# How the first expert gets its rows: gathered from DRAM and turned, or picked out of the resident tiles by one-hot products

## The chip, the cores and the metric

The kernel runs on one core of a Trainium2 chip. A core has five engines with a queue each: TensorE (PE, matrix products; its weight loads are listed apart as PEld), VectorE (DVE), ScalarE (ACT), GpSimd (POOL) and SyncE (SP), and 16 DMA engines. SP issues most of the transfers, and POOL those that need indices or go to late places. The metric is the time of one execution on the device in microseconds (us); lower is better.

## The reference

625 nodes with 768 features go through a layer norm, two graph attention convolutions over 20000 edges and a residual. What the change touches is in the transformer block after it (n = 625 rows, E = 8 experts, K = 1, hidden size 3072):

```python
h = _ln(x, ln1_g, ln1_b)
q, k, v = (jnp.einsum('btd,hds->bhts', h, w) for w in (Wq, Wk, Wv))
scores = jnp.where(causal, jnp.einsum('bhts,bhus->bhtu', q, k) * d ** (-0.5), -jnp.inf)
out = jnp.einsum('bhtu,bhus->bhts', jax.nn.softmax(scores, axis=-1), v)
x = x + out.transpose(0, 2, 1, 3).reshape(b, t, d) @ Wp + bp
h2 = _ln(x, ln2_g, ln2_b).reshape(-1, d)
w, sel = jax.lax.top_k(h2 @ Wg, K)
w = jax.nn.softmax(w, axis=-1)
combine = jnp.zeros((n, E)).at[jnp.arange(n)[:, None], sel].add(w)
hid = jax.nn.relu(jnp.einsum('nd,edf->enf', h2, W1) + b1[:, None, :])
y = jnp.einsum('enf,efd->end', hid, W2) + b2[:, None, :]
return x + jnp.einsum('ne,end->nd', combine, y)
```

(three lines for q, k and v are drawn together here). With K = 1 the weight is a softmax over one value, so it is 1: each row goes through the one expert with its largest gate logit. The kernel computes only that expert for each row, in f32.

## The kernel before, in words

**Tiles.** The 625 rows are T = 5 tiles of R = 125 rows on partitions. D = 768 is KD = 6 blocks of 128. An expert's weights come in NFC = 3 pieces for each layer: `w1[c]` (128 x 6 x 1024) and `w2[c]` (128 x 8 x 768), 3.1 MB each, in two transfers each (`load_piece`, L1300 for the first layer and L1309 for the second). There is one set of these six tiles, so a piece is loaded when the products that read its predecessor are done.

**Attention to gate.** After attention, `project(t, i, cs)` (L1092) multiplies the turned attention output by half i of Wp and adds it to the residual `xx`; `second_norm` (L1113) makes the normalised tile `h2[:, t, :]` (its last DVE operation is L1121). `gate_turn` (`tile_turned`, L1076) turns that tile and `gate` (L1134) multiplies it by Wg; `choose` takes the best expert `ef` and the one-hot row `oh`. `choose_first` counts tile 0's experts. The most frequent one is the **first expert** (`origin`, `first`).

**Routing.** `send(t)` (L1177) counts each row's place within its expert (`pk`, then `rank` and `slot` on DVE), makes its position `pos = expert * RE + slot` (RE = 640, slot from Q = 32 up, L1188) and scatters the rows of `h2` to the DRAM buffer `xg` by an indirect DMA on POOL (L1170). `send_sums` does the same for the residual sums, into `xr`, with the node's number in a last column.

**The first expert ahead of the loop.** While tiles 3 and 4 are not through, the first expert is run on up to B = 128 rows of it from the first TA = 3 tiles. POOL gathers these rows from `xg` into `xa` (L1269) behind the scatters of the three tiles. PE turns `xa` in six blocks with a column stride of 6 (`turn_rows`, L1086), into two PSUM tiles (`tpx`, four and two blocks), copied to `xaT` by DVE and ACT (L1088). This stands behind `gate(3)` and the last products of `project(4, ...)`. POOL also gathers the residual sums into `ra` (L1279), first read when the bias is added (L1424). `first_step` (L1443) then runs the expert with the helpers of `Wide`: `into(c)` (L1372) makes 512 hidden columns in 24 product records, `turn` (L1383, L1388) turns them and adds bias and relu, `out_of(c)` (L1398) multiplies them into the two PSUM banks `pw`. `add_up` adds these to the rows (L1435), `scatter_out` writes them (L1439).

**The loop.** All other rows, in blocks: a table, made on DVE meanwhile, has for each block its expert and kind. The number of blocks is `nblk`. `tc.For_i` (L1695) is a loop on the device, each engine with its own counter. In a block a branch runs `Wide.begin` (the first layer) for 64 or 128 rows, another the narrow form for up to 32 rows (`narrow`, L1649), and then `finish` runs `Wide.end` (the second layer), `add_up` and the scatter. So for wide blocks the branch of the narrow form lies between the two layers.

**What sets the order.** The orders of PE (from attention on), DVE and ACT (from L1228) and SP (L950 to L1694) are the order in which the program is written (`tc.manual_schedule`). Each engine works its queue in order and waits at an instruction until what that reads or overwrites is ready. On SP the loads of the first expert's second and third pieces stand first (L1605 to L1609); then the first loop block's expert word is read, and its loads go out (`load_first`, `load_second`, `load_bias`), then the block count is read into a register on every engine (L1693), and the loop is entered.

Of the kernel before, what the change touches and what calls it, by code (L numbers as in the profile page):

```python
# [9 lines left out]
F32 = mybir.dt.float32  # L10
# [5 lines left out]
OP = mybir.AluOpType  # L16
# [5 lines left out]
R = 125  # L22
T = N // R
XR = 120
D = 768
KD = D // 128
# [17 lines left out]
B = 128  # L44
NS = E + N // B
# [3 lines left out]
Q = 32  # L49
U = B // Q + 1  # L50
TA = 3
RE = 640
# [17 lines left out]
def gnn_moe_kernel(ctx: ExitStack, tc: tile.TileContext, p, out):  # L70
    nc = tc.nc
# [4 lines left out]
    small = ctx.enter_context(tc.tile_pool(name="small", bufs=4))  # L76
# [4 lines left out]
    xg = dram.tile([NR, D], F32, name="xg")  # L81
# [7 lines left out]
                   pattern=[[R, T]], base=0, channel_multiplier=1)  # L89
# [15 lines left out]
    def part(w, k, c, i, n):  # L105
# [4 lines left out]
    ident = const.tile([128, 128], F32, name="ident")  # L110
# [11 lines left out]
                            base=0, channel_multiplier=-1)  # L122
# [32 lines left out]
    with tc.tile_pool(name="gnn", bufs=1) as gp:  # L155
# [37 lines left out]
        with tc.tile_pool(name="oneh", bufs=12) as op_, \  # L193
# [33 lines left out]
            def etile(shape, name, dtype=F32):  # L227
# [4 lines left out]
                           allow_small_or_imprecise_dtypes=True)  # L232
# [399 lines left out]
        with tc.tile_pool(name="gw", bufs=2, reuse_waits="tile") as gw, \  # L632
# [121 lines left out]
            def project(t):  # L754

                for i in range(2):
                    ph = psum_half()
                    for c in range(KH):
                        nc.tensor.matmul(ph[:R, :384], h1T[:, c, cols(t)], part(w2, KH, c, i, 384),  # L759
                                         start=(c == 0), stop=(c == KH - 1))  # L760
                    nc.scalar.copy(xl2[:, t, i * 384:(i + 1) * 384], ph[:R, :384])
                for s, b in enumerate((as2, ad2)):
                    junk = gw.tile([R, HC], F32, tag="hw", name="junk")
                    nc.vector.scalar_tensor_tensor(junk[:, :D], xl2[:, t, :], 1.0, b, op0=OP.mult,
                                                   op1=OP.mult, accum_out=al2[:, s, t, 0:1])
# [97 lines left out]
    with tc.tile_pool(name="att", bufs=1, reuse_waits="tile") as a1, \  # L863
# [58 lines left out]
        for t in range(T):  # L922
# [1 line left out]
            with tc.high_priority() if t < T - 1 else nullcontext():  # L924
                hw = first_norm(t)
            turn(hT, hw, KD, t)
        xa = sx.tile([B, D], F32, tag="xa", name="xa")
        ra = sx.tile([B, D + 1], F32, tag="ra", name="ra")


# [147 lines left out]
                nc.scalar.copy(dst[:, k:k + 3, :], tp[:, :3 * R].rearrange("p (k t) -> p k t", k=3))  # L1078
            return dst

        def turn_rows(dst, src, ps, part, copy):

            k0, k1 = ((0, 4), (4, KD))[part]
            tp = ps.tile([128, 512], F32, tag="tp", name="tpx").rearrange("p (k r) -> p k r", k=4)
            for k in range(k0, k1):
                nc.tensor.transpose(tp[:, k - k0, :],  # L1086
                                    src.rearrange("p (d k) -> p k d", k=KD)[:, k], ident)
            return copy(dst[:, k0:k1, :], tp[:, :k1 - k0, :])  # L1088

        po, stats = {}, {}  # L1090
# [39 lines left out]
        def gate(t):  # L1130
            h2T = h2Ts.pop(t)
            pl = ps.tile([128, 512], F32, tag="tp", name="pl")
            for c in range(KD):
                nc.tensor.matmul(pl[:R, :E], h2T[:, c, :], wg[:, c, :],  # L1134
                                 start=(c == 0), stop=(c == KD - 1))
            nc.vector.tensor_copy(lg[:, t, :], pl[:R, :E])
            choose(t)
# [5 lines left out]
        nc.gpsimd.iota(io8, pattern=[[1, E]], base=0, channel_multiplier=0,  # L1143
                       allow_small_or_imprecise_dtypes=True)
        origin = ap.tile([R, 1], F32, name="origin")

        def best(a):
            mx = small.tile([R, 8], F32, name="mx")
# [9 lines left out]
        def choose_first():  # L1158

            pc = ps.tile([128, 512], F32, tag="tp", name="pc")  # L1160
            nc.tensor.matmul(pc[:R, :E], ones, oh[:, 0, :], start=True, stop=True)
            c0 = small.tile([R, E], F32, name="c0")
            nc.vector.tensor_copy(c0, pc[:R, :E])
            nc.vector.tensor_copy(origin, best(c0))
            nc.vector.tensor_copy(first, origin[0:1, :])

        scatters = {}

        def scatter(buf, src, t):
            s = nc.gpsimd.indirect_dma_start(  # L1170
                out=buf, out_offset=bass.IndirectOffsetOnAxis(ap=pos[t], axis=0),
                in_=src, in_offset=None)
            for q in scatters.setdefault(id(buf), []):
                tc.declare_no_dep(s.ins, q.ins, reason="other rows")
            scatters[id(buf)].append(s)

        def send(t):  # L1177

            pk = ps.tile([128, 512], F32, tag="tp", name="pk")
            for s in range(t + 1):  # L1180
                nc.tensor.matmul(pk[:R, :E], before if s == t else ones, oh[:, s, :],
                                 start=(s == 0), stop=(s == t))
            rank = small.tile([R, E], F32, name="rank")
            slot = small.tile([R, 1], F32, name="slot")
            nc.vector.tensor_tensor_reduce(rank, pk[:R, :E], oh[:, t, :], scale=1.0, scalar=0.0,
                                           op0=OP.mult, op1=OP.add, accum_out=slot)
            nc.vector.tensor_scalar_add(slot, slot, float(Q))
            nc.vector.scalar_tensor_tensor(pos[t], ef[:, t:t + 1], float(RE), slot, op0=OP.mult,  # L1188
                                           op1=OP.add)
            scatter(xg, h2[:, t, :], t)  # L1190

        def send_sums(t):
            nc.vector.tensor_add(x[:, t, :], x[:, t, :], xx[:, t, :])
# [72 lines left out]
        project(3, 1, (2, 3, 4))  # L1266
        send(2)
        first_e = nc.values_load(first[0:1, 0:1], engines=[SP, pool], min_val=0, max_val=E - 1)
        nc.gpsimd.dma_start(xa, xg[ds(first_e * RE + Q, B), :])  # L1269
        for i in range(2):  # L1270
            project(3, i, (KD - 1,))
        turn_probs(last, latest, 1, True)
# [5 lines left out]
            send_sums(t)  # L1278
        nc.gpsimd.dma_start(ra, xr[ds(first_e * RE + Q, B), :])  # L1279
        project(4, 1, most)  # L1280
        gate(3)
        for i in range(2):
            project(4, i, (KD - 1,))
        for part in range(2):
            turn_rows(xaT, xa, ps, part, (nc.vector.tensor_copy, nc.scalar.copy)[part])
        whole_norm(4)
        pe_order.close()

# [23 lines left out]
    def load_bias(e, **cond):  # L1312
        nc.sync.dma_start(b2b, b2[ds(e, 1), :].to_broadcast([B, D]), **cond)
# [24 lines left out]
    def load_first(e, new):  # L1338

        with tc.manual_schedule(engines={SP}):  # L1340
            for c in range(NFC):
                load_piece(e, 0, c, cond=new)

    def load_second(e, new):

        with tc.manual_schedule(engines={SP}):
            for c in range(NFC):
                load_piece(e, 1, c, cond=new)

    class Wide:  # L1350
# [53 lines left out]
        def begin(self):  # L1404
            self.into(0)
            self.into(1)
            for c in range(2, self.n):
                self.turn(c - 2)
                mm = self.into(c)
            return mm  # L1410

# [272 lines left out]
    def word(i, *engines):  # L1684
        return nc.values_load(table[0:1, 0, ds(i, 1)], min_val=0, max_val=2047,
                              **(dict(engines=engines) if engines else {}))

    word_0 = word(0, SP)
    load_first((word_0 >> 8) & 7, (word_0 >> 7) & 1)
    load_second((word_0 >> 8) & 7, (word_0 >> 7) & 1)  # L1690
    load_bias((word_0 >> 8) & 7, cond=(word_0 >> 7) & 1)

    n_blk = nc.values_load(nblk[0:1, 0:1], min_val=1, max_val=NS)  # L1693
    sp_order.close()  # L1694
    with tc.For_i(0, n_blk, 1, iteration_sync="reg_based") as i:  # L1695
        w = word(i)
# [85 lines left out]
```

## Time and profile before

| | us |
|---|---|
| runs | 984.97, 987.18, 987.40; median 987.18 |
| the profiled execution | 986.62 |
| its span, first to last instruction | 984.7 |
| PE busy in 0 to 575 (graph, attention, gate) | 564.2 of 575 |
| PE busy in 575 to 649 (first expert) | 70.6 of 74 |
| PE busy in 649 to 985 (loop) | 314.7 of 336 |
| mean granted clock of TensorE | 0.993 of full |

The profile is one execution. Times in it are us from the span's start; a line number is that of the kernel before. A row of the timeline is a run of like instructions: start, length, engine, line, operation, output <- inputs, shape, count, and in brackets how long the engine was idle before it and what it waited for. An f32 product is recorded twice, as are its weight loads: the 6 products of `gate` are x12. Transposes are recorded once. `PEld`, `SPq`, `DVEq` and the like are weight loads and an engine's own sequencer. The granted clock is the share of full speed at which TensorE was allowed to run.

### The profile page before, as it was taken

The numbers are of one execution on the slowest core, as the hardware profiler recorded it, in microseconds if no ns is written. First come the engines' busy times: TensorE is split into PE (matmuls) and PEld (weight loads), VectorE is DVE, ScalarE is ACT, GpSimd is POOL, SyncE is SP. The second block draws the span as 40 slices with busy tenths as digits, with TensorE's granted clock in tenths as the row PEclk, the third lists the DMA queues.
The fourth block names the chain that finished last, engine by engine and source line by source line (L and its number), as shares of the span: only waits on it lengthen the run. The fifth ranks groups of instructions, "written<-read, shape, count | busy, mean of one in ns | idle before, by whom it ended". The sixth has DMA issues, their size and how long they took to land. (4 is left out here: it accounts for less than half of the span.)

```text
span 984.7 us, 15208 instructions
## 1 busy us (share of the span) xinstructions
PE 949.6 (96%) x4675; PEld 585.8 (59%) x4676; DVE 449.1 (46%) x1310; ACT 296.0 (30%) x776; POOL 65.0 (7%) x147
## 2 busy tenths in 40 slices
PE   8999999999999999999999989999999998999995
PEld 5555665777555556677775655546454656554653
DVE  8978892783384920485555644112111213221303
ACT  6897550562230110444442302101100121011302
POOL 2000000000000100000000113010101010210000
PEclk9999999999999999999999999999999999999998
DMA  9404103001500356999300699310789999999993
GB/s 269 179 1 172 34 1 144 1 1 49 112 1 1 98 144 124 416 400 383 120 1 1 227 346 335 87 43 9 274 291 325 361 366 409 341 396 378 407 404 138
DMA packets 87726, 191.69 MB, mean 195 GB/s; under 512 B 34404, under 2 KB 36316, under 8 KB 87673
## 3 DMA queue, kind: packets, MB, share of 16 engines
q1 hardware_dynamic: 80441, 175.22, 50.1%
q0 software_dynamic: 7152, 15.64, 5.1%
q8 instruction: 29, 0.48, 0.2%
q10 hardware_dynamic: 80, 0.16, 0.1%
q14 instruction: 24, 0.20, 0.1%
HBM read 213.29 MB, written 39.55 MB: 257 GB/s over the span
## 5 line engine op out<-in xcount | busy, mean ns | idle before, releaser
L1398 PE MATMUL pw<-ew,hT 128*64 128x384 f32 (+1 forms) x672 | 159.7, 487 | 4.4 <-DVE iq L1721 2.5
L1398 PEld LDWEIGHTS pw<-ew,hT 128*64 128x64 f32 (+1 forms) x672 | 100.5, 160 | 58.0 <-issue 12.8
L1372 PE MATMUL ph<-ew,xid 128*64 128x512 f32 (+1 forms) x432 | 127.7, 594 | 3.4 <-DMA ew<-in_L_ffn_W_dram 1.8
L1388 ACT ACTIVATE hT<-tph,bT 128x64 f32<-128x64 f32 (+1 forms) x168 | 41.0, 362 | 269.1 <-PE tph L1383 174.4
L1372 PEld LDWEIGHTS ph<-ew,xid 128*64 128x64 f32 (+1 forms) x432 | 53.6, 155 | 66.8 <-issue 59.8
L692 PE MATMUL agg<-xl,zT 125*125 125x256 f32 (+1 forms) x300 | 79.9, 417 | 2.9 <-ACT zT L681 2.9
L1375 DVE COPY hb<-ph 128x512 f32<-128x512 f32 x28 | 19.4, 692 | 137.1 <-PE ph L1372 137.1
L692 PEld LDWEIGHTS agg<-xl,zT 125*125 125x125 f32 x300 | 54.5, 188 | 21.4 <-ACT zT L681 4.4
L1435 DVE TENSOR_TENSOR rw<-rw,pw 64x192 f32<-64x192 f32 (+1 forms) x48 | 12.9, 315 | 90.4 <-PE pw L1398 90.0
L410 PE MATMUL pp<-w,yT 128*125 128x512 f32 x120 | 53.5, 595 | 0.2 <-ACT yT L396 0.2
L800 PE MATMUL ph<-wr,h1T 128*125 128x384 f32 x160 | 52.6, 486 | 0.0
L759 PE MATMUL ph<-w,h1T 128*125 128x384 f32 x160 | 52.4, 486 | 0.0
L256 ACT ACTIVATE step<-halved,past 125x210 f16<-125x210 f16 x138 | 50.9, 460 | 0.0
L1030 DVE CUSTOM_DVE_ANT_0 e<-sc,later 125x625 f32<-125x625 f32 (+4 forms) x60 | 29.9, 543 | 36.2 <-PE sc L1007 36.2
L174 PE MATMUL ph<-wr,yT 128*125 128x512 f32 x96 | 42.2, 594 | 1.0 <-ACT pr L419 0.9
L1034 ACT ACTIVATE e<-e,of 125x625 f32<-125x625 f32 (+4 forms) x60 | 35.7, 597 | 23.3 <-DVE of L1030 23.3
L759 PEld LDWEIGHTS ph<-w,h1T 128*125 128x125 f32 x160 | 30.0, 188 | 21.2 <-issue 0.5
L800 PEld LDWEIGHTS ph<-wr,h1T 128*125 128x125 f32 x160 | 29.8, 188 | 21.1
L1098 PE MATMUL po<-wpj,aT 128*125 128x384 f32 x120 | 41.7, 492 | 0.4 <-DVE xx L1102 0.4
L941 PE MATMUL pv<-L_ffn_Wv,hT 128*125 128x384 f32 x120 | 39.5, 486 | 0.0
L978 PE MATMUL pq<-hT,L_ffn_Wq 128*128 128x313 f32 (+1 forms) x144 | 39.4, 429 | 0.0
L978 PE MATMUL pq<-hT,L_ffn_Wk 128*128 128x313 f32 (+1 forms) x144 | 39.4, 429 | 0.0
(336 smaller groups left out, 1262.3 us busy)
## 6 DMA issues: line engine op xcount, KB each, us to landing
ew<-in_L_ffn_W_dram SPq DMA_DIRECT2D x108, 1536.0 KB
xr<-zt SPq DMA_DIRECT2D x5, 3076.0 KB
xg<-zt SPq DMA_DIRECT2D x5, 3072.0 KB
w<-in_L_gnn_W_dram SPq DMA_DIRECT2D x4, 1536.0 KB
wr<-in_L_gnn_Wr_dram SPq DMA_DIRECT2D x4, 1536.0 KB
xid<-xg POOLq DMA_DIRECT2D x40, 96.0 KB, 9.3
b2b<-in_L_ffn_b_dram SPq DMA_DIRECT2D x9, 384.0 KB
rw<-xr POOLq DMA_DIRECT2D x14, 192.2 KB
```

What stands on the lines that cost most here:

```text
L174: nc.tensor.matmul(pp[:R, :], yT[:, c, cols(t)], part(wr1, KD, c, i, 512), start=(c == 0), stop=(c == KD - 1))
L256: nc.scalar.activation(o, halved[:, :n], AF.Sign, bias=at, scale=-1.0)
L410: nc.tensor.matmul(pp[:R, :], yT[:, c, cols(t)], part(w1, KD, c, i, 512), start=(c == 0), stop=(c == KD - 1))
L692: nc.tensor.matmul(self.agg[:R, c0:c0 + n], zT[:, s, :], xl[:, s, x0:x0 + n], start=(s == 0), stop=(s == T - 1))
L759: nc.tensor.matmul(ph[:R, :384], h1T[:, c, cols(t)], part(w2, KH, c, i, 384), start=(c == 0), stop=(c == KH - 1))
L800: nc.tensor.matmul(ph[:R, :384], h1T[:, k, cols(t)], part(wr2, KH, k, i, 384), start=(k == 0), stop=(k == KH - 1))
L941: nc.tensor.matmul(pp[:R, :384], hT[:, c, cols(t)], w[i][:, c, :], start=(c == 0), stop=(c == KD - 1))
L978: nc.tensor.matmul(pp[:, :b - a], w[:, c, c0:c0 + 128], hT[:, c, a:b], start=(c == 0), stop=(c == KD - 1))
L1098: nc.tensor.matmul(po[t, i][:R, :384], aT[:, c, cols(t)], wpj[i][:, c, :], start=(c == 0), stop=(c == KD - 1))
L1372: mm = nc.tensor.matmul(ph[g * M:(g + 1) * M, :C].rearrange("p (j f) -> p j f", f=128), self.xT[:, k, :], w[:, k, g], start=(k == 0), stop ...
L1388: self.made = nc.scalar.activation(hT[c][:, k, r], tp[:, k, r], AF.Relu, bias=self.bT[:, f:f + 1])
L1398: mm = nc.tensor.matmul(pw[i][g * M:(g + 1) * M, :384], hT[c][:, k, g * M:(g + 1) * M], w[:, self.block(c, g, k), i * 384:(i + 1) * 384], ...
```

## The change

- `xa`, its gather and `turn_rows` go. `pick_rows` stands in their place: for each of the six strided column blocks, three products, one for each of the first three tiles, with the tile's rows of `h2` as weights and `chosen[:, t, :]` (125 x 128) as the moving operand. `chosen` has a one in row r and column c if row r of tile t is row c of the first expert, so the sum of the three products is the block of `xaT` that the turn gave. It stands ahead of `gate(3)`.
- For that, POOL writes a row of column numbers (`io_row`), `choose_first` computes the first expert's first position (`from_row`), and `send(t)` for t < 3 has three more DVE operations: the row's position again, less `from_row`, and the comparison with `io_row`.
- `Wide.begin` gets two 1 x 1 products, one into each bank of `pw`, ahead of its last `into`.
- On SP the block count is read ahead of the first loop block's loads, and the bias load goes ahead of those of the second layer.

```diff
--- before.py
+++ after.py
@@ -924,7 +924,6 @@
             with tc.high_priority() if t < T - 1 else nullcontext():
                 hw = first_norm(t)
             turn(hT, hw, KD, t)
-        xa = sx.tile([B, D], F32, tag="xa", name="xa")
         ra = sx.tile([B, D + 1], F32, tag="ra", name="ra")
 
 
@@ -1078,13 +1077,15 @@
                 nc.scalar.copy(dst[:, k:k + 3, :], tp[:, :3 * R].rearrange("p (k t) -> p k t", k=3))
             return dst
 
-        def turn_rows(dst, src, ps, part, copy):
+        def pick_rows(dst, part, copy):
 
             k0, k1 = ((0, 4), (4, KD))[part]
             tp = ps.tile([128, 512], F32, tag="tp", name="tpx").rearrange("p (k r) -> p k r", k=4)
             for k in range(k0, k1):
-                nc.tensor.transpose(tp[:, k - k0, :],
-                                    src.rearrange("p (d k) -> p k d", k=KD)[:, k], ident)
+                for t in range(TA):
+                    nc.tensor.matmul(tp[:, k - k0, :],
+                                     h2[:, t, :].rearrange("p (d k) -> p k d", k=KD)[:, k],
+                                     chosen[:, t, :], start=(t == 0), stop=(t == TA - 1))
             return copy(dst[:, k0:k1, :], tp[:, :k1 - k0, :])
 
         po, stats = {}, {}
@@ -1143,6 +1144,11 @@
         nc.gpsimd.iota(io8, pattern=[[1, E]], base=0, channel_multiplier=0,
                        allow_small_or_imprecise_dtypes=True)
         origin = ap.tile([R, 1], F32, name="origin")
+        from_row = ap.tile([R, 1], F32, name="from_row")
+        io_row = ap.tile([R, B], F32, name="io_row")
+        nc.gpsimd.iota(io_row, pattern=[[1, B]], base=0, channel_multiplier=0,
+                       allow_small_or_imprecise_dtypes=True)
+        chosen = ap.tile([R, TA, B], F32, name="chosen")
 
         def best(a):
             mx = small.tile([R, 8], F32, name="mx")
@@ -1163,6 +1169,7 @@
             nc.vector.tensor_copy(c0, pc[:R, :E])
             nc.vector.tensor_copy(origin, best(c0))
             nc.vector.tensor_copy(first, origin[0:1, :])
+            nc.vector.tensor_scalar(from_row, origin, float(RE), float(Q), op0=OP.mult, op1=OP.add)
 
         scatters = {}
 
@@ -1188,6 +1195,12 @@
             nc.vector.scalar_tensor_tensor(pos[t], ef[:, t:t + 1], float(RE), slot, op0=OP.mult,
                                            op1=OP.add)
             scatter(xg, h2[:, t, :], t)
+            if t < TA:
+                row = small.tile([R, 1], F32, name="row")
+                nc.vector.scalar_tensor_tensor(row, ef[:, t:t + 1], float(RE), slot, op0=OP.mult,
+                                               op1=OP.add)
+                nc.vector.tensor_sub(row, row, from_row)
+                nc.vector.tensor_scalar(chosen[:, t, :], io_row, row, None, op0=OP.is_equal)
 
         def send_sums(t):
             nc.vector.tensor_add(x[:, t, :], x[:, t, :], xx[:, t, :])
@@ -1266,7 +1279,6 @@
         project(3, 1, (2, 3, 4))
         send(2)
         first_e = nc.values_load(first[0:1, 0:1], engines=[SP, pool], min_val=0, max_val=E - 1)
-        nc.gpsimd.dma_start(xa, xg[ds(first_e * RE + Q, B), :])
         for i in range(2):
             project(3, i, (KD - 1,))
         turn_probs(last, latest, 1, True)
@@ -1278,11 +1290,11 @@
             send_sums(t)
         nc.gpsimd.dma_start(ra, xr[ds(first_e * RE + Q, B), :])
         project(4, 1, most)
+        for part in range(2):
+            pick_rows(xaT, part, (nc.vector.tensor_copy, nc.scalar.copy)[part])
         gate(3)
         for i in range(2):
             project(4, i, (KD - 1,))
-        for part in range(2):
-            turn_rows(xaT, xa, ps, part, (nc.vector.tensor_copy, nc.scalar.copy)[part])
         whole_norm(4)
         pe_order.close()
 
@@ -1406,6 +1418,10 @@
             self.into(1)
             for c in range(2, self.n):
                 self.turn(c - 2)
+                if c == self.n - 1:
+                    for bank in pw:
+                        nc.tensor.matmul(bank[:1, :1], ident[:, :1], ident[:, :1], start=True,
+                                         stop=True)
                 mm = self.into(c)
             return mm
 
@@ -1685,12 +1701,12 @@
         return nc.values_load(table[0:1, 0, ds(i, 1)], min_val=0, max_val=2047,
                               **(dict(engines=engines) if engines else {}))
 
+    n_blk = nc.values_load(nblk[0:1, 0:1], min_val=1, max_val=NS)
     word_0 = word(0, SP)
     load_first((word_0 >> 8) & 7, (word_0 >> 7) & 1)
+    load_bias((word_0 >> 8) & 7, cond=(word_0 >> 7) & 1)
     load_second((word_0 >> 8) & 7, (word_0 >> 7) & 1)
-    load_bias((word_0 >> 8) & 7, cond=(word_0 >> 7) & 1)
-
-    n_blk = nc.values_load(nblk[0:1, 0:1], min_val=1, max_val=NS)
+
     sp_order.close()
     with tc.For_i(0, n_blk, 1, iteration_sync="reg_based") as i:
         w = word(i)
```

## Prediction

> **What bounds the kernel now.** I read the page first, for the engine that is busy all through.
>
> ```profile
> PE 949.6 (96%) x4675; PEld 585.8 (59%) x4676; DVE 449.1 (46%) x1310; ACT 296.0 (30%) x776; POOL 65.0 (7%) x147
> ...
> PE   8999999999999999999999989999999998999995
> ...
> PEclk9999999999999999999999999999999999999998
> ```
>
> TensorE is busy 949.6 of 984.7 us in every slice: the end moves by what is added to its queue, by its idle time, and by its clock. The other engines count only where PE waits for them. So I went to the timeline of the stage that is edited (574 us, where the first expert's rows are fetched and turned):
>
> ```profile
> 571.49 1.37 PE L1134 MATMUL pl<-wg,h2T 128*125 128x8 f32 x12
> ...
> 571.74 0.61 POOL L1269 DMA_DIRECT2D xa<-xg  x1 [9.10 <-DMA xg<-h,pos]
> ...
> 572.72 1.53 PE L1098 MATMUL po<-wpj,aT 128*125 128x384 f32 x4
> ...
> 575.09 1.05 PE L1086 MATMUL tpx<-ident,xa 128*128 128x128 f32 x6 [0.84 <-DMA xa<-xg]
> ...
> 576.99 0.64 DVE L1088 COPY xaT<-tpx 128x512 f32<-128x512 f32 x1
> ...
> 577.68 12.19 PE L1372 MATMUL ph<-ew,xaT 128*128 128x512 f32 x24 [1.55 <-DVE xaT L1088]
> ```
>
> A row is start, length, engine, line, what it does; in brackets the idle time before it and its releaser. PE ends the projections at 574.25 and begins the first expert at 577.68: 3.43 us with 1.05 us of turns in it, the rest waits. Then the table by stretch (length, busy time of PE, PEld, DVE, ACT, POOL, granted clock, DMA share, GB/s), cut where the clock changes, with the second pair of products of the same shape and count (598.96) beside the first:
>
> ```profile
> 577.60:581.00 3.40, 3.32 (x4) 1.51 (x5) 2.04 (x4) 0.06 (x1) 0.00 (x0) 0.50 1.02 373
> ...
> 598.96:609.40 10.44, 10.44 (x28) 4.65 (x26) 8.18 (x67) 0.59 (x1) 2.37 (x2) 1.00 0.94 353
> ```
>
> At the start of the first expert the granted clock is 0.50. The 24 records take 12.19 us there and 10.57 (timeline, 598.96) at full clock. So the stage loses 1.62 us more to the clock than to its gap. Next, the two places outside it: a DVE run ahead of the stage (timeline), and the entry of the loop (timeline and source lines).
>
> ```profile
> 550.12 0.14 DVE L1188 SCALAR_TENSOR_TENSOR pos<-ef,slot 125x1 int32<-125x1 f32 x1
> 550.20 0.79 DVE L1030 CUSTOM_DVE_ANT_0 e<-sc,later 125x625 f32<-125x625 f32 x1
> ...
> 551.65 0.27 DVE L1069 COPY aT<-o 128x125 f32<-128x125 f32 x1
> ...
> 553.44 0.15 DVE L1155 CAST ef<-mi 125x1 f32<-125x1 uint32 x1
> ...
> 553.63 0.23 DVE L1156 TENSOR_SCALAR oh<-io,ef 125x8 bf16<-125x8 f32 x1
> ...
> 553.96 1.02 DVE L1121 SCALAR_TENSOR_TENSOR h<-h,rstd,l2b 125x768 f32<-125x768 f32 x1
> ...
> 555.03 0.86 PE L1076 MATMUL tp<-ident,h 125*128 125x125 f32 x6 [0.36 <-DVE h L1121]
> ```
>
> DVE works without a pause to 554.98, and PE already waits 0.36 us for its last result.
>
> ```profile
> 648.07 0.07 SPq L1313 DMA_DIRECT2D b2b<-in_L_ffn_b_dram  x1
> ...
> L1693 SPq TENSOR_LOAD <-nblk x1: 276/276/276, 648.2 to 648.2; - x1
> ...
> L1695 DVEq EVENT_SEMAPHORE  x2: 21/21/21, 647.8 to 648.0; - x2
> ...
> L1695 SPq EVENT_SEMAPHORE  x21: 17/28/288, 648.8 to 982.4; - x21
> ...
> 649.02 2.37 PE L1372 MATMUL ph<-ew,xid 128*64 128x512 f32 x10 [1.64 <-SPq L1695]
> ```
>
> PE enters the loop 1.64 us after its last product, released by SP's mark at the loop entry. SP is late since its last weight load (issued 647.42, ready only then) is followed by the bias load, the read of the block count (276 ns and 158 to turn it into a number) and only then by its marks at 648.8.
>
> **The change part by part**, against the profiled execution, 986.62 us (span 984.7, 1.9 around it). The median of the runs shown is 987.18, so 0.56 above it; they go from 984.97 to 987.40, and 0.3% (2.96 us) is about what a measurement of this kernel can tell from no change.
>
> *Picks for turns.* Removed: the 3.43 us between projections and first expert, and, if the clock stays up, 1.62 us behind it. Added: 6 column blocks by 3 tiles = 18 products in f32. Each f32 product is recorded twice (the 12 records of the gate for its 6 products), so 36 records. Their weights are h2 read with a stride of 6, as those of the old turns: there six loads start from 575.1 to 575.75, some 0.135 us apart, which is what I take. Lower end 0.109 (record to record of the gate and of the turns of hb, unstrided), upper end 0.24, if load and product (128 columns, half of 256 at 0.216, so 0.107) do not overlap. 36 x 0.135 = 4.86 (3.9 to 8.7). The new order is picks, gate(3) (1.23 to the next stage's start), projections (1.53), first expert: the two copies of the picked rows (0.64 and 0.35) lie beside gate and projections, so PE does not wait for them. The gate takes over the PSUM bank of the first part, but that copy runs beside the second part's 12 records (1.6 us). Stage before, 571.49 to 589.87: 18.38. After: 4.86 + 1.23 + 1.53 + 10.57 = 18.19. So **-0.2** (-1.1 to +5.2, the upper end with the series price and the half clock, 3.8 + 1.6 more).
>
> The half clock is the larger half of that gain: the row gives 0.50 from 577.6 to 581.0, behind 3.43 us with little real work. The Trainium skill (TensorE: Matmul & The Clock Gate, Part 1: The HAM clock gate) says that the gate halves the clock after an idle window of 3.4 us, and that this window runs free of the kernel. This agrees with the stretch's length, and it speaks against the change: the gap of 3.43 us would meet a whole window only by luck of phase, so other executions of before may not pay the 1.62, and against them the stage would cost 1.4 where the row gives -0.2 (sum 988.5 by the rule). [...]
>
> *DVE's new work*, in send(0), (1), (2): row, subtraction, one-hot (125 x 128), and once from_row. Spacings: operations that do not wait for each other 0.08 (550.12 to 550.20), one that reads the last 0.19 (553.44 to 553.63), a copy of 128 x 125 to the next 0.20 (551.65 to 551.85). For tile 0: 0.08 + 0.19 + 0.19 + 0.20 = 0.66, all ahead of the normalisation whose end PE waits for: +0.66. Tile 1: DVE idles 1.88 us at 558.4, so nothing; without that cover 0.58. Tile 2: 0.58, of which a pause of DVE at 561.3 (0.20) and PE's own margin ahead of the turns at 567.58 take some; I take +0.25. Together **+0.9** (0 if PE finds other slack behind it, 1.8 if all three count). These waits are not recovered before the stage, since PE is busy from there on. POOL's new iota runs long before.
>
> *POOL.* The gather and its wait of 9.10 us for the scatters leave POOL's queue; the scatters of the sums behind it and the gather of ra come earlier. ra is first read at 633.59, so nothing is gained or lost; only the transfers lie closer to the weights.
>
> *Weight loads of the first expert.* The second pieces (issued 574.39 and 576.50) take space that the last projections' operands free; projections end some 5.5 us later, near 580. 3.1 MB at the 373 GB/s of the row are 8.4 us: first piece in at 589, needed at 599, the next in at 597, needed at 620. Hidden; without that cover at most 5.5 us.
>
> *SP's order.* Block count read first (0.44 on SP, before loads for 611 that PE needs at 649), and the bias ahead of the second weight loads. The bias tile is free only when DVE has read it at 633.59 + 0.95, so loads that were issued at 631.65 now go at 634.6: first use 666.8, covered by some 15 us at the DMA share of 0.16 there. At loop entry SP has its marks right behind the load at 647.42: 647.6. Next late is DVE, whose two marks end at 647.98; PE then starts near 648.1 in place of 649.02: **-0.9** (-1.26 if DVE's marks are early too, 0 if SP still trails).
>
> *Dummies.* Two 1x1 f32 products in each of 6 wide blocks (432 records of the expert's first layer by 72): 24 records of 0.025 (the one-column products of the first stage) to 0.109, so 0.6 to 2.6. I take 0.03: 0.7, of which waits for weight DMAs later in the loop take a third: **+0.45** (0 to +2.6). What would they take away? In the loop PE idles at the second layer's start:
>
> ```profile
> PE pw L1398 <- DVE iq L1721: 2.5, 2, 1.4
> ...
> PE pw L1398 <- PEq L1718: 1.3, 2, 0.7
> ```
>
> These (list of PE's waits in the loop: us, times, longest) are 2.5 + 1.3 = 3.8 us at four starts. The DVE addition that frees the two banks is done over 15 us earlier, two of the four are put down to PE's own branch, so I take no gain from here.
>
> Sum: 986.62 - 0.2 + 0.9 - 0.9 + 0.45 = **986.9**.
>
> **The rivals.**
> - *Slower: strided picks run in series.* If load and product of a pick don't overlap, a record costs 0.24, 36 x 0.105 = 3.8 more: 990.7. For it: all 36 share two PSUM banks and accumulate by threes. Against: the old turns, same load shape, ran at 0.135. It decides from 0.225 a record (986.9 + 36 x 0.09 = 990.1).
> - *Faster: the dummies empty the waits at the branch.* 3.8 us go for 0.7: 986.9 - 0.45 - 3.1 = 983.4. For it: half is labelled DVE. Against: that DVE work is long done.
> - *Faster: nothing shows of the additions.* Picks at 0.109 (-0.95), DVE's work hidden (-0.9), and the later half-clock stretch (816.5 to 819.9, some 1.7 us of PE) not met after the shift: 983.4. Against: PE's recorded wait at 555.03.
> - *Slower: late weights.* The second pieces come 5.5 us later and meet the scatters of 580 to 600, where DMA is full (share 1.0): if the slack of 10 us is used up, up to 5.5, most likely two thirds of it: 990.6; with the whole, 992.4. It decides from 3.2 us of waits at the first expert's later products.
> - *The clock stays halved* at the first expert since picks don't keep it up: +1.6, 988.5, within the bound.
>
> **How the numbers follow.** As summed, with the terms near the values taken and with the clock case: 0.40 (own range 985.0 to 988.9). Series 0.17; late weights 0.13, of it 0.08 over the bound; dummies 0.14; additions hidden 0.16. Faster by over 0.3% (below 984.2): 0.14 + 0.16 = 0.30. Slower (above 990.1): 0.17 + 0.08 = 0.25. Same: 0.40 + 0.05 = 0.45. The range runs from a little under the two fast cases, 982.8, to a little over the series case, 991.2, which leaves out the tails of the fast and the slow cases, under 0.2.
>
> **What would show it.** Right: picks of 36 records in some 4.9 us with no idle time before the gate; clock 1.00 at the first expert and 24 records in 10.6; PE's wait for h before the turns of tile 2 grown from 0.36 to about 1.0; loop entry idle about 0.7, put down to DVE; waits at the second layer's starts still about 3.8. Wrong: record spacing near 0.24; a wait of the third pair of products for a weight DMA; the starts of the second layer without a gap.

## The result, and the profile after

The changed kernel is **slower**: 991.55 us, median of five runs (990.26 to 992.49), against 986.63 for the kernel before on the same chip (984.97 to 987.40). The ratio is 1.0058 with a 95% interval of 1.0045 to 1.0070. Beside later experiments, on another occasion, it was 990.09 against 986.44: 1.0038 (1.0024 to 1.0051). So it costs between a quarter and two thirds of a percent, some 4 us. The profiled execution took 991.57 us, with a span of 989.3 (before: 986.62 and 984.7).

The page after, engines and slices:

```profile
PE 953.9 (96%) x4729; PEld 591.8 (60%) x4730; DVE 450.9 (46%) x1320; ACT 295.9 (30%) x776; POOL 64.6 (7%) x147
...
PE   8999999999999999999999999999999998989995
...
PEclk9999999999999999999999999999999999999998
```

TensorE has 4.3 us more to do (953.9 for 949.6), although the half-clock stretch at the first expert is gone; its share of the span is the same. So the loss is, in sum, work and not waiting. The timeline of the stage says which work (start, length, engine, line, what it does):

```profile
572.66 8.06 PE L1086 MATMUL tpx<-chosen,h 125*128 125x128 f32 x36
580.56 1.38 PE L1135 MATMUL pl<-wg,h2T 128*125 128x8 f32 x12
581.79 1.53 PE L1099 MATMUL po<-wpj,aT 128*125 128x384 f32 x4
583.16 10.46 PE L1384 MATMUL ph<-ew,xaT 128*128 128x512 f32 x24
```

and the instructions of the picks' PSUM tile (duration in ns, min/median/max):

```profile
L1086 PEld LDWEIGHTS tpx<-chosen,h x36: 297/317/318, 572.3 to 580.2; 125*128 125x128 f32 x36
```

The 36 pick records take 8.06 us, 0.224 us a record, and PE waits for nothing on the way: neither gap nor half clock is left. (From the first pick's start to the gate's it is 7.90, so 0.22 from one start to the next.) The gate and the projections took the same as before, and the first expert 10.46. From the start of the stage to the end of the first 24 records before took 18.38 us; now it is 20.96 (572.66 to 593.62). That is +2.6 at this place alone.

The other places that the prediction named, in the timelines of after:

```profile
555.92 0.86 PE L1075 MATMUL tp<-ident,h 125*128 125x125 f32 x6 [0.95 <-DVE h L1122]
...
568.76 0.83 PE L1075 MATMUL tp<-ident,h 125*128 125x125 f32 x6 [0.39 <-DVE h L1122]
...
651.87 1.51 PE L1384 MATMUL ph<-ew,xid 128*64 128x512 f32 x6 [0.73 <-DVEq L1711]
...
662.90 0.24 PE L1423 MATMUL pw<-ident 128*1 128x1 f32 x4
```

and the turns of tile 3 in the timeline of before:

```profile
567.58 0.84 PE L1076 MATMUL tp<-ident,h 125*128 125x125 f32 x6
```

PE's wait for the normalised tile 2 has grown from 0.36 to 0.95, a wait of 0.39 stands ahead of the turns of tile 3, where the row of before had none, the loop entry's wait has shrunk from 1.64 to 0.73 and is now put down to DVE, and the 1x1 products take some 0.2 a block. And in the loop (waits of PE, in us, times, longest):

```profile
PE pq L1688 <- DMA ew<-in_L_ffn_W_dram: 3.3, 2, 3.1
PE pw L1410 <- DVE iq L1737: 2.5, 2, 1.5
PE ph L1384 <- DMA ew<-in_L_ffn_W_dram: 1.8, 2, 1.0
PE pw L1410 <- DMA ew<-in_L_ffn_W_dram: 1.5, 1, 1.5
PE pw L1410 <- PEq L1734: 1.4, 2, 0.7
```

The waits at the starts of the second layer (2.5 and 1.4) are as they were. What is new is a wait of 1.5 us for weights.

Laid side by side, the same instruction of the two traces is later in after by: +0.88 at the turns of tile 2, +1.18 at those of tile 3, +3.75 at the end of the first expert's first 24 records, +2.84 at the loop's first product, +3.62 at the wide block that starts at 764.79, and +4.6 at the end of the span. Of all these 0.24 was there before any of the new work: at 545 us, where the gate of an earlier tile begins at 545.40 for 545.16. So DVE's new work makes 0.65 at the turns of tile 2 and 0.95 with those of tile 3, as the waits say too (0.59 and 0.39 more). The expectations below count the 0.24 in, have 1.18 for DVE's part, and call these the turns of tiles 0 and 2.

### The profile page after: what moved, and what is told of

It reads as the page before. It is cut to its first block, busy times and chain, and to the rows that moved or that the text cites. A ratio compares the mean times of both kernels' runs of the same rounds, so it can differ in the third digit from the quotient of the medians.

```text
span 989.3 us, 15327 instructions
## 1 busy us (share of the span) xinstructions
PE 953.9 (96%) x4729; PEld 591.8 (60%) x4730; DVE 450.9 (46%) x1320; ACT 295.9 (30%) x776; POOL 64.6 (7%) x147
```

## The experiments

Two theories stood at the start. **Theory 1**: the terms read from after's trace add up: the picks with their strided weights, DVE's work, the dummies (the 1x1 products), less SP's order. **The rival**: the loop, whose weight stream is full from about 755 us on, makes or takes back part of it. A third question was why a pick costs 0.224.

### The parts, one by one

The kernel before with the picks alone: the diff of the change without the two pieces below, SP's order and the 1x1 products.

> The kernel before with the picks alone (no dummies, SP's order as it was). In the trace of after the 36 pick records are 0.224 us apart and the stage costs 2.6 us more than the gather, turns and half clock did, and DVE's new work delays the turns of tile 0 and tile 2 by 0.89 and 0.29. Theory 1, these terms hold and add up: first expert 3.75 later, loop entered 3.7 to 4.0 later, and the weight stream in the loop gives about as much or 1 more: 990.3 to 991.5. Rival, the loop's extra wait for weights in after (1.2 us) comes from SP's new order or the dummies: then here the loop adds nothing and the time is 990.3 +- 0.3, with the loop's waits for weight DMAs as before.

Measured: 991.57 against 986.58, ratio 1.0051 (1.0033 to 1.0069). Its profiled execution is one of its shorter ones, 989.92: there the first 24 records end 3.27 later than in before, the loop is entered as much later, as SP still trails, and the loop itself adds nothing. So the picks with DVE's work alone make a loss of the size of the whole change's.

SP's order alone, on the kernel before:

```diff
+    n_blk = nc.values_load(nblk[0:1, 0:1], min_val=1, max_val=NS)
     word_0 = word(0, SP)
     load_first((word_0 >> 8) & 7, (word_0 >> 7) & 1)
+    load_bias((word_0 >> 8) & 7, cond=(word_0 >> 7) & 1)
     load_second((word_0 >> 8) & 7, (word_0 >> 7) & 1)
-    load_bias((word_0 >> 8) & 7, cond=(word_0 >> 7) & 1)
-
-    n_blk = nc.values_load(nblk[0:1, 0:1], min_val=1, max_val=NS)
```

> The kernel before with only SP's order changed. Theory 1: the loop entry's idle time of PE goes from 1.64 to about 0.7 and nothing takes it back: 985.7. Rival: the bias ahead of the second layer's loads holds those back and the weight stream of the loop, which is full from about 755 us on, takes the 0.9 back: 986.6, or later if the loop waits for weights 1 us more.

Measured: 986.07 against 986.58, ratio 0.9998 (0.9985 to 1.0012): the 0.9 that was expected lies inside the interval and can't be told from nothing by the times. The trace shows it: PE's wait at the entry is 0.73 and put down to DVE. It also shows something that was not looked for. The stage ahead of the first expert is that of before, with a wait at the turns and at the products, yet the 24 records run in 10.57 us:

```profile
575.90 1.05 PE L1086 MATMUL tpx<-ident,xa 128*128 128x128 f32 x6 [1.12 <-DMA xa<-xg]
...
578.20 10.57 PE L1372 MATMUL ph<-ew,xaT 128*128 128x512 f32 x24 [1.26 <-DVE xaT L1088]
...
647.01 6.23 PE L1372 MATMUL ph<-ew,xid 128*64 128x512 f32 x28 [0.73 <-DVEq L1695]
```

So the half clock of before's profiled execution is not a fixed property of its code. This profiled execution (984.39 us) is 2.2 under that of before: 0.9 at the entry and 1.6 at the clock, less 0.5 by which it is late already ahead of them.

The 1x1 products alone, on the kernel before, and the changed kernel without them (the same lines taken out):

```diff
                 self.turn(c - 2)
+                if c == self.n - 1:
+                    for bank in pw:
+                        nc.tensor.matmul(bank[:1, :1], ident[:, :1], ident[:, :1], start=True,
+                                         stop=True)
                 mm = self.into(c)
```

> The kernel before with only the two 1x1 products a wide block. Theory 1: each block's first layer is some 0.17 us longer, so what comes ahead of the full weight stream (three blocks) costs about 0.5 and the later ones nothing: 987.1. Rival, they trigger a later weight stream and are behind the 1.2 us that the loop loses in after: 988.3. Rival, they take away the waits at the second layer's starts: 983.4.

> The changed kernel without the 1x1 products. Theory 1: 0.5 less than after: 991.0. Rival, they are behind the loop's extra wait for weights: 989.8.

Measured: 986.74 against 986.58, ratio 1.0003 (0.9992 to 1.0014), and 989.47 against 986.58, 1.0030 (1.0017 to 1.0042). On before they cost nothing that can be told. Taken out of after they seem worth 2 us beside its first five runs, but only 0.6 beside its repeat. That time fits the rival's 989.8, and the loop of this trace lost nothing, so these runs alone do not refute the rival; a run further below speaks against it. The traces put some 0.2 us on each of the blocks. That they take waits away is refuted: the waits at the second layer's starts are there with and without them. Here too, in the profile of the one on before, the first expert's 24 records ran at full clock (10.57 us) behind the same turns:

```profile
578.10:588.60 10.50, 10.50 (x28) 4.71 (x29) 2.58 (x4) 0.00 (x0) 0.00 (x0) 1.00 1.01 382
```

(table by stretch: length, busy time of PE, PEld, DVE, ACT, POOL, granted clock 1.00, DMA share, GB/s.)

The changed kernel was also run a second time beside the last experiments:

> The changed kernel once more, beside the others on one chip. Theory 1, its parts: picks 8.06 for 5.05 or 3.43 (with or without a half clock at the first expert in before), DVE 1.18, SP's order -0.9, dummies 0.5: 3.8 to 5.4 over before of this chip. Rival, the 1.2 us that its loop lost to a wait for weights in its profile belong to that execution: then nearer 3.8.

Measured: 990.09 against 986.44, 1.0038 (1.0024 to 1.0051), the lower end of what the terms give. Its trace has the pick stage again at 8.06 and the loop entry at 0.73; from 764 us, where it is 3.24 later than before, to its end it loses another 1.0. So the loop's loss came in both profiles of this kernel and, with 1.6, in that of the kernel with the longest picks (below); the ten other kernels tried lie between 0.6 less and 0.5 more over the same stretch. What makes it was not settled.

### What makes a pick cost 0.224

Contiguous column blocks as weights:

```diff
-                                     h2[:, t, :].rearrange("p (d k) -> p k d", k=KD)[:, k],
+                                     h2[:, t, k * 128:(k + 1) * 128],
```

> The changed kernel with the picks' weights read as contiguous column blocks of h2 instead of every sixth column; nothing else changes (the first expert then gets its features in another order than its weights have, so this leaves the right order out). Theory 1, the strided reading of the weights paces the picks: records go from 0.224 us apart to about 0.11 (the gate's contiguous loads), the pick stage from 8.06 to about 4.0, and the time to 4.1 less than after: 987.4. Rival, load and product of a pick run in series (0.109 + 0.107 = 0.216 from contiguous rows): records stay near 0.216 and the time within 0.4 of after: 991.2.

Measured: 986.25 against 985.90, ratio 1.0002 (0.9993 to 1.0011): nearly all of the loss is gone. Its timeline:

```profile
572.62 4.18 PE L1086 MATMUL tpx<-chosen,h 125*128 125x128 f32 x36
576.64 1.38 PE L1135 MATMUL pl<-wg,h2T 128*125 128x8 f32 x12
```

36 records from 572.62 to 576.64, where the gate begins, are 0.112 apart, half of the strided price (7.90 us counted in the same way), at the same shape and count. The series rival needed 0.216 here and falls. That leaves the weight load with the stride of 6, and one more way to put it: perhaps load and product overlap only when the load is contiguous. For that, each pick was cut into two products of 64 moving columns:

```diff
-                for t in range(TA):
-                    nc.tensor.matmul(tp[:, k - k0, :],
-                                     h2[:, t, :].rearrange("p (d k) -> p k d", k=KD)[:, k],
-                                     chosen[:, t, :], start=(t == 0), stop=(t == TA - 1))
+                for c in (slice(0, 64), slice(64, B)):
+                    for t in range(TA):
+                        nc.tensor.matmul(tp[:, k - k0, c],
+                                         h2[:, t, :].rearrange("p (d k) -> p k d", k=KD)[:, k],
+                                         chosen[:, t, c], start=(t == 0), stop=(t == TA - 1))
```

> The changed kernel with each pick as two products of 64 moving columns, so 72 records with the same strided weights. Theory 1a, the strided weight load alone takes 0.224 and the product is hidden behind it: records stay 0.224 apart, the pick stage 16.1, 8.1 more than after. Theory 1b, with strided weights load (0.112) and product (half as long, 0.053) run in series: records 0.165 apart, the stage 11.9, 3.8 more than after.

Measured: 1002.66 against 986.44, ratio 1.0158 (1.0140 to 1.0176). The timeline and, below it, two stretches of the table by stretch (columns as above):

```profile
572.11 16.08 PE L1087 MATMUL tpx<-chosen,h 125*128 125x64 f32 x72
587.99 2.63 PE L1136 MATMUL pl<-wg,h2T 128*125 128x8 f32 x12
```

```profile
572.50:575.50 3.00, 3.00 (x15) 3.00 (x15) 0.00 (x0) 0.00 (x0) 1.22 (x2) 1.00 0.46 103
577.00:587.00 10.00, 10.00 (x47) 10.00 (x46) 0.69 (x1) 0.00 (x0) 0.61 (x1) 0.50 0.30 94
```

72 records in 16.08: 0.223 apart with half the columns. Both theories took their prices at full clock, so the stretch at 1.00 decides: there 15 records touch 3.00 us, and at 0.165 apart it would be 18 or more. So the strided load alone sets the pace, and the product is hidden behind it: theory 1a. The run was 12.6 over after's repeat where 8.1 were expected. Of the other 4.5 the clock makes about 4.3, by the profiled execution. From about 576 us it is 0.50, through gate (2.63 for 1.38) and projections (2.90 for 1.53) and into the first expert (its 24 records take 12.13 for 10.46). PE and PEld are recorded as busy all the time.

### DVE's new work, and versions that keep the idea

The one-hots made later, ahead of the sums, for the three tiles together:

```diff
-            if t < TA:
-                row = small.tile([R, 1], F32, name="row")
...
-                nc.vector.tensor_scalar(chosen[:, t, :], io_row, row, None, op0=OP.is_equal)
...
+        nc.vector.tensor_scalar(from_row, origin, float(RE), float(Q), op0=OP.mult, op1=OP.add)
+        nc.vector.scalar_tensor_tensor(rows_, ef[:, :TA], float(RE), slots, op0=OP.mult, op1=OP.add)
+        nc.vector.tensor_scalar(rows_, rows_, from_row, None, op0=OP.subtract)
+        for t in range(TA):
+            nc.vector.tensor_scalar(chosen[:, t, :], io_row, rows_[:, t:t + 1], None, op0=OP.is_equal)
         for t in range(TA):
             send_sums(t)
```

> The changed kernel with DVE's new operations (from_row, row, subtraction, the three one-hots) issued ahead of the sums of tiles 0 to 2, where DVE idles before the picks in after (571.4 to 578.1), instead of in send. Theory 1: the turns of tile 0 and tile 2 go back to the times of before, the picks start 1.2 earlier, 990.3. Rival: PE then waits at the picks for the last one-hot, and the 1.2 comes back there: 991.5.

Measured: 989.24 against 985.90, ratio 1.0031 (1.0019 to 1.0043). In its trace the wait is that of before again, and the picks start at 571.60 for 572.66, without a wait for the one-hots:

```profile
555.15 0.86 PE L1075 MATMUL tp<-ident,h 125*128 125x125 f32 x6 [0.36 <-DVE h L1122]
...
567.69 0.84 PE L1075 MATMUL tp<-ident,h 125*128 125x125 f32 x6
...
571.60 8.06 PE L1086 MATMUL tpx<-chosen,h 125*128 125x128 f32 x36
```

Of this 1.06, 0.12 was there at 545 us; DVE's work cost the other 0.95. By the times, 1.0031 lies below both results of after (1.0058 and 1.0038); its interval ends just under that of the first and overlaps that of the second. The same without the 1x1 products:

> The changed kernel with DVE's new work issued late and without the 1x1 products. Theory 1: against the run with the late DVE work alone 0.5 less, 2.6 over before. Rival, the 1x1 products cost 2 (as the run without them suggests beside after): 1.2 over before.

Measured: 989.34 against 986.44, ratio 1.0033 (1.0021 to 1.0045), level with the run above. So the 2 us that the 1x1 products seemed to be worth were not there; they cost less than these runs can tell.

The rows picked untransposed, with the one-hots as contiguous weights, and turned afterwards; then the same with DVE's work late and without the 1x1 products:

```diff
+            for t in range(TA):
+                nc.tensor.matmul(tp[:, :384], chosen[:, t, :], h2[:, t, c], start=(t == 0),
+                                 stop=(t == TA - 1))
+            return copy(dst[:, c], tp[:, :384])
...
         gate(3)
+        for part in range(2):
+            turn_rows(xaT, xa, ps, part, (nc.vector.tensor_copy, nc.scalar.copy)[part])
```

> The changed kernel with the picks the other way round: the one-hots are the weights (contiguous, 128 columns) and h2 moves by 384 columns, which gives the rows untransposed (6 products, 12 records at the 0.322 of other 384-column products, 3.9 us); they are copied to SBUF and turned with the stride of 6 as before (6 transposes at 0.135, 0.8 us) behind the gate of tile 3. Theory 1, the strided weights of f32 products are what is slow: 4.7 in place of 8.06 on PE, 988.1. Rival, the copies between picks and turns put a wait of 1 us or more on PE: 989.1 or later.

> Rows picked untransposed as in the run of that kind, DVE's new work issued late, SP's new order, no 1x1 products. By the terms of theory 1: against before, the stage costs 0.8 more (4.7 for the turns' 1.05 and 2.4 of waits, when the half clock does not fall on the first expert) or 0.8 less (when it does), DVE nothing, SP's order 0.9 less: 985.0 to 986.5, so a little under before. Rival, the shorter path only meets the full weight stream of the loop earlier and waits there: as before, 986.6.

Measured: 987.05 against 985.90, ratio 1.0009 (1.0000 to 1.0018), and 986.18 against 985.90, 1.0001 (0.9992 to 1.0010). The 12 records of the first take 4.04, and the turns wait 0.35 for DVE. So the loss is gone but for 0.1%, and with the other repairs the kernel is level with before, but not better.

Last, contiguous weights in the right order: ScalarE copies the three tiles of h2 into contiguous blocks in its idle time, and the picks read these. (The copies lie in `xaT` and, as `hp`, in the space of `xa` and `ra`, so the gather of `ra` goes out behind the picks.) With DVE's work late, SP's order, and no 1x1 products:

```diff
         gate_turn(2)
+        for t in range(TA):
...
+            nc.scalar.copy(hp[t][:R], h2[:, t, :].rearrange("p (d k) -> p k d", k=KD))
...
-                                     h2[:, t, :].rearrange("p (d k) -> p k d", k=KD)[:, k],
+                                     hp[t][:R, k, :],
```

> Late DVE work, no 1x1 products, SP's new order, and ScalarE copies the three tiles of h2 into six contiguous blocks each (in 557 to 564, where it idles), from which the picks read their weights. Theory 1, contiguous weights at 0.112 a record: picks 4.06, first expert 1.1 earlier than with the untransposed rows, which was level with before: 1.0 under before. Rival, the loop's full weight stream takes it back: level with before.

Measured: 984.46 against 986.44, ratio 0.9986 (0.9977 to 0.9995). It is the one version here that beats both kernels, by 2 us at the medians. Its picks run with 0.111 from one record to the next:

```profile
571.41 0.39 PE L1085 MATMUL tpx<-chosen,xaT 125*128 125x128 f32 x2
571.64 0.61 PE L1085 MATMUL tpx<-chosen,hp 125*128 125x128 f32 x4
572.08 0.39 PE L1085 MATMUL tpx<-chosen,xaT 125*128 125x128 f32 x2
```

(six records from 571.41 to 572.08), and the gate starts at 575.43.

How much of the 2 us comes from the picks is not shown. From the turns of tile 2 to the end of the first 24 records it takes 33.54 us (554.96 to 588.50). Before's profiled execution takes 34.84 (555.03 to 589.87), but the two executions of the old stage at full clock take 33.2 (555.56 to 588.77 with SP's order alone, 555.36 to 588.60 with the 1x1 products alone). So against the old stage at full clock the contiguous picks are 0.3 longer, and against the one at half clock 1.3 shorter. SP's order, which is in this version too, makes another 0.9 in the traces.

## Why the prediction was wrong

It forecast no change, 986.9, and put 0.25 on slower. The time was 991.55 and slower by more than the 0.3% bound. Step by step:

- *Picks for turns: the step that failed.* The price of a record was taken from the old turns, 0.135, since they load with the same stride. It was 0.22: from the first pick to the gate 7.90 us where 4.86 were put in, 3.0 us more, which is most of the miss. The nearest row in stride was the wrong one, as a transpose's strided load is cheaper than that of an f32 product; with contiguous weights the two are alike (0.109 for the turns of `hb`, the first layer's output, 0.112 for picks). The upper end, 0.24, was near the truth, and so was the rival that carried it, with 990.7, and the point given for it, 0.225. But its mechanism was wrong: load and product do overlap (the 64-column run), and it is the load that is slow.
- *The half clock.* The trace of after has 1.00 there, as said, and the 24 records take 10.46. But the 1.62 us that this was worth were credited against one execution. Two other executions with the old stage, shown above, did not have it; against them the new stage costs 4.2 (20.96 for 16.8 from the gate to the end of the 24 records), not 2.6. The Trainium skill (TensorE: Matmul & The Clock Gate, Part 1: The HAM clock gate) says that the window of the gate runs free of the kernel and that the effect varies from run to run; these runs agree, at 12.19 us in one execution and 10.57 in two. The prediction weighed this rule and did not follow it in the sum.
- *DVE's new work.* Predicted +0.9, and the wait before tile 2's turns at about 1.0; the trace has +0.95, 0.65 ahead of tile 2's turns and 0.30 ahead of tile 3's, and that wait at 0.95. Size and mechanism were right, and the late version confirms it.
- *SP's order.* Predicted -0.9, idle 0.7 and put down to DVE: the trace shows 0.73 for 1.64, by DVE. Right.
- *Dummies.* Predicted 0.7 on PE without taking a wait away, +0.45 in sum. The waits are still there, as said; a block's first layer is 0.17 longer in the trace (11.21 for 11.04), so some 1.0 for six blocks; in the times they can't be told from nothing.
- *POOL and the later weight loads.* Costed at nothing; after's trace has no wait of the first expert for its second pieces, so the rival of late weights didn't come.
- *The loop.* The prediction let everything ahead of it shift it rigidly. After's profiled execution lost one more us in the full weight stream, and so did its repeat, where ten other kernels lost up to 0.5 or gained up to 0.6. In this stretch (from 764.79 to the end, 761.17 in before) PE waits 20.45 us for 18.22 in before, and is busy 1.15 less: the half clock of before at 816.5 to 819.9 does not come (clock 1.00). That part of the rival in which nothing shows of the additions came true, and gave nothing, as waits took its place. The new wait of 1.5 for weights does not explain the loss: the executions with SP's order alone and with the 1x1 products alone have one of 1.9 in its place and no longer loop. Nor does the wait of the narrow form's first products for weights: it is 3.1 in after, 2.5 in its repeat and 1.8 and 1.6 in those two, but 2.4 in the last version above, whose loop is no longer either. This part of the miss stays open.

Sum on the profiled execution's own time, with the measured terms: 986.62 + 0.24 (there at 545 us already) + 0.95 (DVE) + 2.57 (stage) - 0.91 (SP) + 0.78 (loop up to 764.79: three times 0.17 for the 1x1 products, the rest not assigned) + 1.0 (loop) = 991.25, where 991.57 was measured; the rest lies outside the span. The terms are the steps by which one trace falls behind the other, so that they add up proves none of them.

## What to carry to other kernels

Price a TensorE operand by its layout and by its kind together: the row of a transpose does not price the weight load of an f32 product with the same stride, and where only such a row is at hand, give the far end its weight (here it was the right one). If a strided weight operand can't be avoided, let an idle engine make it contiguous first, as ScalarE did here: 4.0 us from the first pick to the gate for 7.9. Do not credit a clock dip of one profile: see whether other executions of the same code have it.

## What the runs showed of the hardware that was not expected

- An f32 product's weight load with 128 columns at a stride of 24 bytes takes 0.22 us a record, against 0.112 contiguous. The Trainium skill (TensorE: Matmul & The Clock Gate, LDWEIGHTS (loading the stationary operand)) gives columns/1.2 ns for a load, by which 128 columns are an estimated 107 ns: the contiguous picks agree, and the strided ones cost double. The strided loads of the transposes took 0.135. Why the two differ was not tried.
- That pace does not follow the granted clock: in the run with 64 columns the records stay 0.22 apart at 1.00 and at 0.50. The contiguous loads of the gate do follow it: its 12 records take 1.38 us at 1.00 and 2.63 at 0.50.
- The clock fell to 0.50 in that run while PE and PEld were recorded as busy without a pause. With 128 moving columns at the same pace it did not (1.00 in after). All four executions of that run have a lower mean clock (0.984 to 0.987) than those of after's repeat (0.994 to 0.997). So a recorded busy share of 100% did not keep the clock up.
